# Quarters instead of halves: layer norms, adaptive scale and shift, and residual sums of an eight-stage transformer chain

## The chip, the cores and the metric

The kernel runs on one core of a Trainium2 chip. The metric is the device time of one execution in microseconds; the time before is 1702.09, the median of three runs (1697.55 to 1703.14). All arithmetic is in float32. A core has a tensor engine (PE, with its weight loads PEld), a vector engine (DVE), a scalar engine (ACT), GpSimd (POOL) and a queue that issues DMAs (SP). Matrix products land in PSUM; the rest of the data is in SBUF, 128 partitions wide.

## The reference, cut to what matters

1024 tokens (16 batches of 64) with 128 features pass through eight stages, each on the layer norm of the sum so far (residual):

```python
x = x + L0_xcond(_layernorm(x), cond, ctx)  # an attention decoder, recurrent over the 64 positions
x = x + L0_ffn(_layernorm(x))               # MoE, 8 experts, top 2, a shared expert, layer norm at its end
x = x + L1_xcond(ctx, _layernorm(x), cond)  # perceiver attention, 16 heads
x = x + L1_ffn(_layernorm(x))               # gated feed-forward with fake quantisation
x = x + L2_xcond(_layernorm(x), cond, ctx)  # six layers, below
x = x + L2_ffn(_layernorm(x))               # MoE, 8 experts, top 2
x = x + L3_xcond(_layernorm(x), cond, ctx)  # one block: two attentions of 16 heads, gated feed-forward
x = x + L3_ffn(_layernorm(x))               # MoE, 8 experts, top 2
```

The part that the change touches most is the adaptive layer norm, which the reference of the six layers writes as

```python
def _adaln(x, emb, w, b):
    gb = emb[:, 0, :] @ w.T + b
    g, be = jnp.split(gb, 2, axis=-1)
    return _ln(x) * (1.0 + g[:, None, :]) + be[:, None, :]
```

Scale and shift differ by batch and feature. Each layer applies it three times: before self attention, before cross attention and before the feed-forward. A few stages norm an input that is already a norm (the residual starts from `_ln(x)`), so that the second norm can be worked out from the first one's statistics; the kernel calls that "twice".

## The kernel before, in words

**Stages and planner.** Each stage builds a list of operations (`plan.op(engine, ns, emit, deps, takes, on, peers)`): the engine, an estimated duration, a function that emits the instructions, what must be done before, and a buffer that it takes. A greedy planner (`_Plan.order`) repeatedly emits, of all ready operations, the one that can start first by these durations; among equals the one with the longest remaining chain behind it goes first. Every engine then runs its instructions in the order of emission. The planner's durations only set the order: the waits between engines are put in afterwards, from what the instructions read and write. `peers` order starts only; `on` says that an operation works in another's buffer.

**Tiling.** Tokens lie on partitions in eight groups of 128 (`NT`). All planned stages work by halves of the tokens (512, four groups), `h` = 0 and 1, whose operations the planner interleaves. A half of feature-major data is one PSUM tile of 128x512, a whole bank. PSUM buffers of the layers: `pj` two tiles for nearly every product and transpose, `S` one of four banks for scores, `O` one of two banks for attention outputs. The block and the perceiver have four `pj`. The MoE stages have three `pj`, three `y`, two `tp`.

**A norm of a half** (`half_stats`, `half_scaled`, `half_features`, `adaln_half`): DVE takes statistics of four groups (L2137), aggregates them (L2143) and adds epsilon (L2144); POOL raises to the power -1/2 (L2148, four columns); DVE works out the shift (L2150); two groups are scaled by ACT (L2179) and two by DVE (L2177) into `xn`; PE transposes all four into one PSUM tile (L2192); DVE multiplies it by the scale into `xT` (L2202, 128x512) and POOL adds the shift (L2204). Every user of `xT` waits for that POOL addition.

**Attention in the layers** (`attend_half`): q, its rotated copy, k and v are projected from `xT` through `pj`; DVE and POOL rotate (L2218, L2221); ACT and DVE spread q into `qx` by masks (L2266, L2268); PE makes scores into `S`, ACT exponentiates (L2300), PE makes outputs into `O`, in four groups `p`, of which 0 and 1 lie in the first bank of `O` and 2 and 3 in the second. After groups 0 and 1, and again after 2 and 3, DVE takes reciprocals (L2309) and normalises (L2313), PE transposes, ACT copies, PE projects, and DVE adds to the residual (L2326), each time for a quarter of the tokens. The second add waited for the first (`last`), and the next norm waits for the second.

**Feed-forward of the layers** (`ffn_half`): four products with gelu on ACT (L2346), then `project`, one operation of 16 products into one `pj` tile, then one DVE add over the half (L2359). `glu_half` of the block does the same with a gate.

**MoE** (`moe`): for each expert and half four up-projections with activation, four down-projections (one per token group, 0.9 us each in the planner) into one `y` tile, and `weigh`: four DVE operations (L1674), one per group, that add the tile times the router's weight to the accumulator. `weigh` waits for all four down-projections.

**Heads of block and perceiver** (`heads_half`): the output projection is four operations of eight products into one `pj` tile, then one DVE add (L1884).

**Layers' start.** `norm_half` (L1331 to L1344) norms the stage's input into the residual, emitted before the plan; the first layer's norm then starts from that result.

Of the kernel before, what the change touches and what calls it, by code (L numbers as in the profile page):

```python
# [1140 lines left out]
class _Plan:  # L1141
# [13 lines left out]
    def op(self, engine, ns, emit, deps=(), takes=None, on=None, peers=(), table=None):  # L1155
# [3 lines left out]
        o.k, o.users, o.slot = len(self.ops), [], None  # L1159
        deps = list({id(d): d for d in deps if d is not None}.values())  # L1160
# [84 lines left out]
class _Fast(_Net):  # L1245
# [319 lines left out]
    NORM = (("st", 4, [128, 4, 6]), ("mv", 4, [128, 4, 3]), ("rs", 4, [128, 4, 6]), ("xn", 2, [128, 4, D]))  # L1565
# [3 lines left out]
    def moe(self, name, act, gated=False, shared=False):  # L1569
# [7 lines left out]
        with ExitStack() as st:  # L1577
# [29 lines left out]
            for h in range(2):  # L1607
                t = self.half_features(self.half_norm(half(x0, h), None), "tp")
                xTs.append(plan.op("ACT", 600, lambda _, h=h, t=t: nc.scalar.copy(
                    xT[:, h * 512:(h + 1) * 512], t.slot[1]), [t]))  # L1610
# [22 lines left out]
            for h in range(2):  # L1633
# [3 lines left out]
                for e in ([E] if shared else []) + list(range(E)):  # L1637
# [28 lines left out]
                    def weigh(y, e=e, h=h, acc=acc, first=last is None):  # L1666
                        for k in range(4):
# [9 lines left out]
                    last = plan.op("DVE", 1300, weigh, [*downs, None if e == E else route, last], on=y)  # L1677
                    if e == 1:
                        t = plan.op("PE", 870, lambda t, h=h: self.mm(t, cT, bd[:, h * 512:(h + 1) * 512]), [cTo], "tp")
                        last = plan.op("DVE", 690, lambda _, t=t, acc=acc: nc.vector.tensor_tensor(  # L1680
                            acc.rearrange("p k d -> p (k d)"), acc.rearrange("p k d -> p (k d)"), t.slot[1], ALU.add),
                            [t, last])
                if shared:
# [4 lines left out]
                    xa, xb = self.half_norm(acc, last)  # L1688
                    g = plan.op("DVE", 690, lambda t: nc.vector.tensor_tensor(t, t, row("ln_g"), ALU.mult),
                                [xa, xb], on=xa)  # L1690
                    plan.op("DVE", 690, lambda _, h=h, g=g: nc.vector.tensor_tensor(
                        half(x, h), half(x, h), g.home.slot[1], ALU.add), [g, base])
# [63 lines left out]
    def heads_half(self, h, x, wq, wk, wv, wo, inv, q, ks, vs, many, bias, top):  # L1756
# [118 lines left out]
        ys = []  # L1875
# [8 lines left out]
        return plan.op("DVE", 690, lambda t: nc.vector.tensor_tensor(flat, flat, t, ALU.add), [*ys, top], on=y)  # L1884

    def perceiver(self):
# [5 lines left out]
        with ExitStack() as st:  # L1892
# [12 lines left out]
            wide = [128, 8, T]  # L1905
            view = lambda v: v.rearrange("p (b t) -> p b t", t=T)
            deps = []
            for h in range(2):
                bs, part = slice(h * 8, (h + 1) * 8), slice(h * 4, (h + 1) * 4)
                t = self.half_features(self.half_norm(self.ctx[:, part, :], None))  # L1910
                c = plan.op("DVE", 690, lambda _, t=t, bs=bs: nc.vector.tensor_scalar(
                    kvT[:, bs, 0, :], view(t.slot[1]), w("ln1_w"), w("ln1_b"), ALU.mult, ALU.add), [t])
                xh = x0[:, part, :]
                t = self.half_features(self.half_scaled(xh, self.half_stats(xh, None, True)[1], 3))
                l = plan.op("DVE", 690, lambda _, t=t, bs=bs: nc.vector.tensor_tensor(
                    kvT[:, bs, 1, :], view(t.slot[1]), a[:, bs].unsqueeze(2).to_broadcast(wide), ALU.mult), [t])
                l = plan.op("POOL", 1060, lambda _, bs=bs: nc.gpsimd.tensor_tensor(
                    kvT[:, bs, 1, :], kvT[:, bs, 1, :], b[:, bs].unsqueeze(2).to_broadcast(wide), ALU.add), [l])
# [17 lines left out]
    def block(self):  # L1936
# [4 lines left out]
        with ExitStack() as st:  # L1941
# [13 lines left out]
            for h in range(2):  # L1955
# [6 lines left out]
                once, twice = self.half_stats(x0h, None, True)  # L1962
                firsts.append(self.half_scaled(x0h, twice, 3))
                xa, xb = self.half_scaled(x0h, once, 0, xh)
# [165 lines left out]
    def half_stats(self, x, top, twice=False):  # L2130
# [22 lines left out]
        if not twice:  # L2153
            return once
# [276 lines left out]
```

## Time and profile before

| what | us |
|---|---|
| median of the three runs | 1702.09 |
| the profiled execution, whole | 1709.73 |
| its span, first to last instruction | 1707.9 |
| stretch 0 to 230: decoder | PE busy 197.6 |
| 230 to 374: first MoE | PE busy 130.4 of 144 |
| 374 to 526: perceiver | PE busy 144.9 of 152 |
| 526 to 594: quantised feed-forward | PE busy 38.8 of 68 |
| 594 to 1218: six layers | 624 |
| 1218 to 1346: second MoE | 128 |
| 1346 to 1573: block | PE busy 215.6 of 227 |
| 1573 to 1708: third MoE and end | PE busy 122.0 of 135 |

One layer in the middle takes 95.6 us (886.6 to 982.2), of which PE is busy 82. A matrix product of 128x512 takes 0.59 us in the record and about 1.2 where the granted clock of the tensor engine is 0.5; the clock is given as a share of full speed. Products are pipelined, so that the records of two in a row overlap.

How to read the profile: a group or timeline line names the engine, the line of the kernel, the operation, the tile written and the tiles read, shapes and count; in brackets stands how long the engine had been idle before and which engine's instruction ended that. L295 is the line of a helper that issues every product, so products are told apart by their tiles. The windows give busy time of each engine in a stretch, and the mean clock. The list of waits gives, for an engine, the total of idle times that a certain instruction of another engine ended.

### The profile page before, as it was taken

To read this page: it belongs to the slowest core of one execution; us is meant where nothing else is said; L and a number is where in the kernel's file an instruction comes from. 1 tells how busy PE (TensorE), PEld (TensorE's weight loads), DVE (VectorE), ACT (ScalarE), POOL (GpSimd) and SP (SyncE) were. 2 spreads that over 40 slices of the span, in tenths; PEclk is the share of its full clock that TensorE was granted. 3 is DMA by queue.
4 is the path that set the end of the run, shared out by engine and by line. 5 is a ranking of instruction groups with operands and counts; after the bars stand their busy time and mean duration, and the time that the engine had idled before them with its cause. 6 is when DMAs were issued, how large, how long until landed. Compare 5 with 4: busy or idle time off the path is not lost.

```text
span 1707.9 us, 46734 instructions
## 1 busy us (share of the span) xinstructions
PE 1510.6 (88%) x21223; PEld 1113.3 (65%) x21223; DVE 711.0 (42%) x2217; ACT 533.6 (31%) x885; POOL 206.3 (12%) x210
## 2 busy tenths in 40 slices
PE   6999979969996698888798888888899899998997
PEld 5888857757774256566566556566567678775675
DVE  4434441243335565545646554444311343443212
ACT  2111134433321123333343333323343333332432
POOL 0000000020000032312222231212100200001000
PEclk7555569989997689989999897765799899999999
DMA  6000000000000040101000000000300200000000
GB/s 219 4 4 4 5 1 1 1 1 1 2 2 9 12 174 17 29 16 30 16 7 16 16 16 12 19 2 2 131 7 1 100 2 2 2 2 1 1 1 15
DMA packets 14332, 38.41 MB, mean 22 GB/s; under 512 B 1682, under 2 KB 6674, under 8 KB 14125
## 3 DMA queue, kind: packets, MB, share of 16 engines
q1 hardware_dynamic: 14125, 35.34, 6.1%
q8 instruction: 168, 2.75, 0.7%
q14 instruction: 39, 0.32, 0.1%
HBM read 34.81 MB, written 0.52 MB: 21 GB/s over the span
## 4 chain that ended last, share of the span: by engine, by line
PE 59%; DVE 11%; issue 3%; POOL 2%; ACT 2%; DMA 0%; DVEq 0%; ACTq 0%; POOLq 0%; SPq 0%
PE pj L295 35%; PE O L295 8%; PE y L295 7%; PE S L295 6%; DVE qx L2268 2%; DVE u L2218 1%; PE pj L1865 1%; DVE st L2137 1%; ACT P L2300 1%; POOL xT L2204 1%; POOL rs L2148 1%; DVE mv L2144 1%; PE pj L2319 1%; PE tp L295 1%; DVE xT L2202 1%
## 5 line engine op out<-in xcount | busy, mean ns | idle before, releaser
L295 PEld LDWEIGHTS y<-m_sb,H 128*128 128x128 f32 x1568 | 185.8, 192 | 32.5 <-issue 31.3
L295 PE MATMUL pj<-xT,m_sb 128*128 128x512 f32 x392 | 189.6, 618 | 0.0
L295 PE MATMUL y<-m_sb,H 128*128 128x128 f32 x1568 | 186.0, 275 | 0.0
L2300 ACT ACTIVATE P<-S 128x1024 f32<-128x1024 f32 x96 | 98.1, 1022 | 164.1 <-PE S L295 164.1
L1650 ACT ACTIVATE H<-pj,m_sb 128x512 f32<-128x512 f32 x128 | 87.5, 687 | 130.6 <-PE pj L295 130.3
L295 PEld LDWEIGHTS pj<-xT,m_sb 128*128 128x128 f32 x392 | 72.2, 199 | 63.3 <-issue 63.1
L2148 POOL TENSOR_TENSOR rs<-mv,minus_half 128x4 f32<-128x4 f32 x54 | 56.2, 1045 | 464.9 <-DVE mv L2144 463.8
L1674 DVE SCALAR_TENSOR_TENSOR x<-y,cw,x 128x128 f32<-128x128 f32 x128 | 36.0, 344 | 174.6 <-PE y L295 174.6
L2218 DVE TENSOR_TENSOR u<-pj,consts_sb 128x512 f32<-128x512 f32 x96 | 65.7, 688 | 68.7 <-PE pj L295 68.0
L2179 ACT ACTIVATE xn<-x,rs 128x128 f32<-128x128 f32 x100 | 43.4, 485 | 95.4 <-DVE rs L2150 78.4
L295 PE MATMUL pj<-xT,w_sb 128*128 128x512 f32 x128 | 66.3, 639 | 3.5 <-POOL xT L2204 3.1
L1775 DVE COPY QKV<-pj 128x512 f32<-128x512 f32 x56 | 38.6, 690 | 73.9 <-PE pj L295 73.8
L295 PE MATMUL pj<-xT,l_f 128*128 128x512 f32 x96 | 56.7, 720 | 13.7 <-POOL xT L2204 6.0
L295 PE MATMUL cb<-bd,E 128*32 128x2 f32 x4096 | 64.9, 192 | 2.9 <-issue 2.9
L1650 ACT ACTIVATE H<-pj,b1g,m_sb 128x512 f32<-128x512 f32 x64 | 49.6, 777 | 53.8 <-PE pj L295 50.8
L295 PEld LDWEIGHTS O<-Vc,P 128*64 128x64 f32 x1536 | 59.5, 163 | 10.4 <-issue 8.3
L295 PE MATMUL O<-Vc,P 128*64 128x18 f32 x1536 | 64.5, 230 | 0.0
L295 PEld LDWEIGHTS cb<-bd,E 128*32 128x32 f32 x4096 | 62.5, 156 | 3.0 <-issue 3.0
L2204 POOL TENSOR_TENSOR xT<-xT,ada 128x512 f32<-128x512 f32 x42 | 43.7, 1042 | 169.0 <-DVE xT L2202 130.7
L2192 PE MATMUL pj<-consts_sb,xn 128*128 128x128 f32 x184 | 36.4, 334 | 28.5 <-POOL rs L2148 14.6
L295 PE MATMUL S<-qx,krc 32*64 32x128 f32 x1536 | 42.0, 338 | 21.4 <-DVE qx L2268 17.8
L295 PE MATMUL O<-Vs,P 128*64 128x18 f32 x1536 | 55.4, 217 | 5.4 <-DVE On L2313 5.4
(363 smaller groups left out, 2617.2 us busy)
## 6 DMA issues: line engine op xcount, KB each, us to landing
w_sb<-in_w SPq DMA_DIRECT2D x7, 681.5 KB, 8.3
m_sb<-in_m SPq DMA_DIRECT2D x8, 515.0 KB, 6.6
m_sb<-in_m SPq DMA_DIRECT2D x8, 514.5 KB, 6.1
m_sb<-in_m SPq DMA_DIRECT2D x7, 565.5 KB, 9.4
l_f<-in_l SPq DMA_DIRECT2D x6, 578.5 KB, 3.9
l_a<-in_l SPq DMA_DIRECT2D x6, 387.0 KB, 3.1
l_s<-in_l SPq DMA_DIRECT2D x6, 384.0 KB, 3.2
w_sb<-in_w SPq DMA_DIRECT2D x4, 512.5 KB, 11.6
```

The lines of the kernel that those rows point to most:

```text
L295: self.nc.tensor.matmul(out, lhsT=lhsT, rhs=rhs, start=start, stop=stop, **kw)
L1650: nc.scalar.activation(a[:, c, :], ups[c].slot[1], act, bias=b, scale=g)
L1674: nc.vector.scalar_tensor_tensor(acc[:, k, :], src, g, x0[:, i, :] if first else acc[:, k, :], ALU.mult, ALU.add)
L1775: e(o, i.rearrange("p (b t) -> p b t", t=T) if len(o.shape) == 3 else i)
L1865: t = plan.op("PE", 700, lambda t, On=On: [nc.tensor.transpose(t[:, i * 128:(i + 1) * 128], On.slot[1][:, i * 128:(i + 1) * 128], self.ide ...
L2148: rs = plan.op("POOL", 1030, lambda t: nc.gpsimd.tensor_tensor(t[:, :, 0], at(mv, 2), self.minus_half[:, 0:4], ALU.pow), [mv], "rs")
L2179: nc.scalar.activation(o, x[:, k, :], AF.Identity, bias=b, scale=r)
L2192: return self.plan.op("PE", 900, lambda t: [self.nc.tensor.transpose(t[:, k * 128:(k + 1) * 128], xa.slot[1][:, k, :], self.ident) for k i ...
L2204: return plan.op("POOL", 1060, lambda a: nc.gpsimd.tensor_tensor(view(a), view(a), part(2 * n + 1), ALU.add), [m, ada], on=m)
L2218: us.append(plan.op("DVE", 690, lambda u, t=t, k=k, table=table: nc.vector.tensor_tensor(view(u[:, k, :]), view(t.slot[1]), self.c(table). ...
L2268: nc.vector.tensor_scalar(o, r, m, None, ALU.mult)
L2300: P = plan.op("ACT", 1030, lambda P, S=S: nc.scalar.activation(P.rearrange("p (g c) -> p g c", g=4), S.slot[1][:, :, 0:256], AF.Exp, scale ...
```

## The change

- `half_stats`, `half_scaled` and `adaln_half`'s two operations go. A new `quarter_norm` norms two token groups: statistics, aggregates and epsilon as one DVE operation, the power on POOL over two columns, the shift on DVE, then one group on ACT and one on DVE. With `twice` it also gives the second norm's factors; with `out` the first norm's result is written as well.
- `half_features` transposes by quarters into the two halves of one PSUM tile and calls `use` for each. `adapted` is that use for adaptive norms: for each batch of 64 tokens one operation `x * scale + shift` with the scale and shift as columns, read from PSUM, two batches of a quarter on ACT and two on DVE. POOL's addition goes.
- The residual sums of `ffn_half` and `glu_half` (new `add_quarters`), of `heads_half`, and the MoE's `weigh` are split in two, each waiting for its own products; norms wait for the add of their quarter. In the attention of the layers the second add no longer waits for the first.
- In the layers `norm_half` goes; the residual's start is written by `quarter_norm` with `out`, inside the plan. The perceiver, the block and the MoE's last norm use the same functions.

```diff
-    NORM = (("st", 4, [128, 4, 6]), ("mv", 4, [128, 4, 3]), ("rs", 4, [128, 4, 6]), ("xn", 2, [128, 4, D]))
+    NORM = (("nq", 6, [128, 2, 16]), ("xn", 4, [128, 2, D]))
...
-                    last = plan.op("DVE", 1300, weigh, [*downs, None if e == E else route, last], on=y)
+                    last = [plan.op("DVE", 650, lambda y, j=j, weigh=weigh: weigh(y, j), [
+                        *downs[2 * j:2 * j + 2], None if e == E else route, last and last[j]], on=y)
+                        for j in range(2)]
...
-        return plan.op("DVE", 690, lambda t: nc.vector.tensor_tensor(flat, flat, t, ALU.add), [*ys, top], on=y)
+        for k in range(2):
+            cut = slice(k * 256, (k + 1) * 256)
+            adds.append(plan.op("DVE", 420, lambda t, cut=cut: nc.vector.tensor_tensor(
+                flat[:, cut], flat[:, cut], t[:, cut], ALU.add), [*ys[2 * k:2 * k + 2], top], on=y))
+        return adds
...
+    def add_quarters(self, x, project, deps, base):
+        nc, plan = self.nc, self.plan
+        flat, t, adds = x.rearrange("p k d -> p (k d)"), None, []
+        for q in range(2):
+            cut = slice(q * 256, (q + 1) * 256)
+            o = plan.op("PE", 1800, lambda t, q=q: project(t, q), deps, None if q else "pj", on=t, peers=[t])
+            t = t or o
+            adds.append(plan.op("DVE", 420, lambda _, cut=cut: nc.vector.tensor_tensor(
+                flat[:, cut], flat[:, cut], t.slot[1][:, cut], ALU.add), [o, base]))
+        return adds
...
-            for h in range(2):
-                self.norm_half(x0, h, xs[h])
-            tops = [None, None]
+            qs = [[self.quarter_norm(x0[:, h * 4:(h + 1) * 4, :], k, None, True, xs[h]) for k in range(2)]
+                  for h in range(2)]
+            tops = [[o for _, o in qs[h]] for h in range(2)]
...
+    def quarter_norm(self, x, k, top, twice=False, out=None):
+        xk = x[:, 2 * k:2 * k + 2, :]
+        def stats(t):
+            for i in range(2):
+                nc.vector.bn_stats(out=t[:, i, 0:6], in_=xk[:, i, :])
+            for i in range(2):
+                nc.vector.bn_aggr(out=t[:, i, 6:8], in_=t[:, i, 0:6])
+            nc.vector.tensor_scalar(t[:, :, 8], t[:, :, 7], EPS, None, ALU.add)
...
+        q = plan.op("DVE", 1060, stats, [top], "nq")
+        r = plan.op("POOL", 1030, power(8, 9), [q], on=q)
+        once = plan.op("DVE", 180, shift(9), [r], on=q) if not twice or out is not None else None
...
+        n = plan.op("ACT", 480, lambda t: scaled("ACT", 0, at, t[:, 0, :]), [rs], "xn")
+        n = [n, plan.op("DVE", 350, lambda t: scaled("DVE", 1, at, t[:, 1, :]), [rs], on=n, peers=[n])]
...
+    def half_features(self, ns, use, kind="pj"):
+        plan, t, ops = self.plan, None, []
+        for k, n in enumerate(ns):
+            def transpose(t, k=k, n=n):
+                for i in range(2):
+                    at = (2 * k + i) * 128
+                    self.nc.tensor.transpose(t[:, at:at + 128], n[0].slot[1][:, i, :], self.ident)
+            o = plan.op("PE", 450, transpose, n, None if k else kind, on=t, peers=[t])
+            t = t or o
+            ops += use(k, lambda: t.slot[1], o)
+        return ops
...
+            for j, engine in enumerate(("ACT", "DVE")):
+                def run(a, j=j, engine=engine):
...
+                    for b in (2 * j, 2 * j + 1):
+                        f = scale()[:, 4 * k + b:4 * k + b + 1], shift()[:, 4 * k + b:4 * k + b + 1]
+                        if engine == "DVE":
+                            nc.vector.tensor_scalar(o[:, b, :], i[:, b, :], *f, ALU.mult, ALU.add)
+                        else:
+                            nc.scalar.activation(o[:, b, :], i[:, b, :], AF.Identity, bias=f[1], scale=f[0])
...
+                o = plan.op(engine, 700 if engine == "ACT" else 460, run, [t, ada], take if first else None,
...
-            last = plan.op("DVE", 420, lambda _, xv=xv, t=t: nc.vector.tensor_tensor(
-                xv, xv, t.slot[1][:, :256], ALU.add), [t, last])
+            adds.append(plan.op("DVE", 420, lambda _, xv=xv, t=t: nc.vector.tensor_tensor(
+                xv, xv, t.slot[1][:, :256], ALU.add), [t]))
...
-        t = plan.op("PE", 3550, project, [*hs, load], "pj")
-        flat = x.rearrange("p k d -> p (k d)")
-        return plan.op("DVE", 690, lambda _: nc.vector.tensor_tensor(flat, flat, t.slot[1], ALU.add), [t, xb])
+        return self.add_quarters(x, project, [*hs, load], xb)
```

## The prediction

> **What bounds the kernel now.** First the page, then busy time by stage, then the tensor engine's waits in the longest stage, then that stage's timeline.
>
> ```profile
> span 1707.9 us, 46734 instructions
> PE 1510.6 (88%) x21223; PEld 1113.3 (65%) x21223; DVE 711.0 (42%) x2217; ACT 533.6 (31%) x885; POOL 206.3 (12%) x210
> ```
>
> PE is the bound, with little room. The windows (columns: stretch, PE, PEld, DVE, ACT, POOL busy, clock, DMA) show where the room lies: the six layers, one MoE stage, and one moment of a layer.
>
> ```profile
> 594.00:1218.00 624.00, 537.28 (x8096) 370.68 (x8096) 323.56 (x931) 209.18 (x306) 157.87 (x148) 0.87 0.09 26
> 1218.00:1346.00 128.00, 124.13 (x689) 90.39 (x689) 29.27 (x113) 48.52 (x74) 2.19 (x5) 0.96 0.13 50
> 906.00:910.00 4.00, 2.68 (x9) 1.32 (x10) 3.74 (x8) 0.88 (x2) 2.06 (x3) 1.00 0.00 0
> 946.00:949.40 3.40, 0.00 (x1) 0.01 (x1) 3.30 (x9) 0.72 (x1) 2.52 (x2) 0.71 0.25 95
> 949.40:958.00 8.60, 8.41 (x104) 5.20 (x104) 2.15 (x5) 2.93 (x4) 1.07 (x2) 0.52 0.01 2
> ```
>
> The layers leave PE idle for 87 us and run at a mean clock of 0.87; the MoE stage is 97% PE. At 946.0 PE does nothing for 3.4 us, and the next 8.6 us run at half clock. What ended PE's waits in the layers (total, times, longest):
>
> ```profile
> PE S L295 <- DVE qx L2268: 22.2, 11, 3.5
> PE pj L295 <- POOL xT L2204: 13.0, 14, 3.0
> ...
> PE O L295 <- DVE On L2313: 5.4, 5, 1.1
> PE pj L2319 <- DVE xT L2202: 4.9, 9, 0.6
> ```
>
> The first is that 3.4 us hole: the scores of the cross attention's first half wait for a chain that starts at the self attention's last add. Its ends in the timeline:
>
> ```profile
> 934.54 0.42 DVE L2326 TENSOR_TENSOR x<-x,pj 128x256 f32<-128x256 f32 x1 [2.19 <-PE pj L295]
> 934.88 0.86 DVE L2137 BATCH_NORM_STATS2 st<-x 128x6 f32<-128x128 f32 x4
> ...
> 941.77 1.04 POOL L2204 TENSOR_TENSOR xT<-xT,ada 128x512 f32<-128x512 f32 x1 [4.37 <-DVE xT L2202]
> ...
> 949.40 1.16 PE L295 MATMUL S<-qx,krc 32*64 32x128 f32 x32 [3.50 <-DVE qx L2268]
> ```
>
> The third wait matters for the change. The O tile holds four groups of outputs; the reciprocal (L2309) needs groups 0 and 1 alone, group 3 needs nothing of it:
>
> ```profile
> 924.69 2.05 PE L295 MATMUL O<-Vs,P 128*64 128x18 f32 x64
> ...
> 926.78 0.36 DVE L2309 RECIPROCAL inv<-O 128x32 f32<-128x32 f32 x1 [2.80 <-PE O L295]
> 927.17 0.49 DVE L2313 TENSOR_TENSOR On<-O,inv 128x128 f32<-128x128 f32 x2
> ...
> 927.81 1.11 PE L295 MATMUL O<-Vs,P 128*64 128x18 f32 x32 [1.07 <-DVE On L2313]
> ```
>
> The x64 is groups 1 and 2. DVE waits for group 2, and group 3 waits for DVE: writers and readers of one PSUM tile go in program order, whatever columns they touch. The change makes quarters inside PSUM tiles, so this is priced throughout.
>
> **The change, part by part** (us; plus is slower).
>
> Norm chain, from the last add to xT. Now: statistics and aggregates 1.3 (0.86, then 0.36 overlapping, 0.17), power 1.02 with 0.25 of hops, shift 0.24, two ACT rows 0.87, hop 0.15, transposes 0.66, xT multiply 0.69, POOL add 1.04, hops 0.2: 6.4; the trace took 7.85 from 934.96 to 942.81. After, for the last quarter: 0.9 for half the statistics, power 1.27 with hops, 0.24, one ACT row 0.48, 0.15, two transposes 0.44, then the feature scale and shift in pieces of 64 columns. On ACT such a piece is 0.43: the xn row 128x128 at 0.485 less 64 columns of 0.9 ns (copies of 512 and 256 columns: 0.586 and 0.368); two in a row 0.76. On DVE it is 0.28, a second 0.20 later, from the 0.344 and the spacing of L1674's four (1.12 together): 0.48. No row has ACT and DVE read one tile at once; side by side it is 0.76, in order 0.76+0.1+0.48. I take in order, as the O tile goes. Sum 4.9: a gain of 1.5. The power of 2 columns instead of 4 is not shown: 0.51 (half) to 1.02; I take 1.02, the nearer row's. Where is it exposed? In the hole at the cross attention's first half, six times: **-9** (-4 to -14).
>
> After the feed-forward both adds come together. The second quarter's transposes then wait for the first quarter's readers: add 0.8, statistics to 1.75, first transposes done at 4.25, its readers at 5.75, second at 7.8, against 7.2 now. One half per layer has no cover: 6 x 0.6 = **+3.6** (-9 to +8).
>
> The clock. Idle of 3.4 us was followed by 8.41 us of PE work at half clock, which is 4.2 lost; with holes of 1.0 to 1.2 us at 906 the clock stayed at 1.00. A hole of 3.4-1.5 = 1.9 lies between; I take half of it over five layers: **-10.5** (0 to -21). The Trainium skill (TensorE: Matmul & The Clock Gate, HAM oscillation) says that only idle beyond about 3.4 us drops the clock; by that rule alone this term would be -21.
>
> MoE sums by halves of y. L1674's four operations become two and two, the first pair due after two of four down projections. The planner places it between the third and the fourth. In program order it waits for the third, and the fourth waits for it: 0.05+0.61+0.15 = 0.8 of PE idle in a stage without slack. That happens only where the four run back to back. With halves, the chain of sums costs 690 per expert by the planner's numbers instead of 1340, so in the second half an up-projection two experts ahead outranks the down projections and splits them, as in the first half now. What is left is the last three experts and the one at the bias matmul: 4 or 5 per stage, 14 in all: **+11** (0 to 39, all 49 groups). The last sum of a stage is half as long: **-1.5**.
>
> Output projections of the heads: the first add falls between the third and fourth block: 0.05+0.42+0.15 = 0.6, six halves: **+3.6** (0 to 3.6). Feed-forward sums by quarters: PE writes both before DVE's first add, which waits for both; two adds take 0.8 instead of 0.69: 14 x 0.1 = **+1.4**. That part does not do what it says.
>
> pj in the layers has two buffers. Now xT's tile is held for 0.66+0.1+0.69+0.15 = 1.6. After, from the first quarter's transposes to the second's readers: the adds lie 2.6 apart (931.93, 934.54), plus 0.44+0.1+0.76+0.1+0.48: 4.5, or 2.8 times. PE waits today 4.9+1.5 = 6.4 for that reader; the increase is 1.8 x 6.4 = **+11.5** (0 to 23).
>
> DVE and ACT. Per half DVE gives up 0.69 and gets 0.96 of pieces and a second shift and epsilon (0.2 each in a row): +0.6. It also waits for ACT's two pieces, 0.86 per quarter; u, qx and the adds stand behind it. ACT gets 4 x 0.4 and, at 31% busy, hides it; if exponentials stand ahead, DVE waits longer. DVE is the bound only in 906 to 910 (3.74 of 4 us), one half a layer: 6 x 2.3 = 13.8. Against it: small DVE operations stall behind the POOL add (mv at 904.60 took 0.83 against a median of 0.17, ending with it); that excess is 4.6 in the kernel, and no such excess lies under a power. **+9** (0 to 14). POOL itself trades one add for a second power, 1.04 for 1.02, in the slack of a 12% engine.
>
> Stage starts: MoE's first norm about 1 earlier, three times: **-3**. Norms taken twice (perceiver, block, layers) need eight powers instead of four, but the first half needs four either way: 0. The layers' own first norm (L1331 to L1344, emitted ahead of the plan) moves into it and shares its statistics: eight statistics of 0.28 and their aggregates less on DVE between 595 and 602, behind them the masks that POOL's V columns wait for; PE is then mostly waiting for weights (half clock, DMA landing), so 0. All three together -10 to +8.
>
> Sum: -9+3.6-10.5+11-1.5+3.6+1.4+11.5+9-3 = +16. The profiled execution took 1709.7, 1.8 more than its span, and is 7.6 above the median; on the median of 1702.1 that is **1718**.
>
> The skill speaks against this change: PSUM — Partial Sum Buffer (PSUM bank collisions raise a hardware error) has two engines on one bank ordered by semaphores, two readers included. The O rows agree for PE and DVE; for two readers no run here shows it. Without that rule for readers, the chain gains 0.58 more, -3.5 over six layers.
>
> **Rivals.** *The clock holds (faster).* If the hole falls under the 1.2 us that 906 shows harmless, the clock term is -21, and the last half layer, at 0.63 from 1125 to 1218, gains too: 0.74 of its 80 us of PE time is at half clock, 59, so 30 are lost; half of that back is -15. 1718-10.5-15 = **1692**; with pj and DVE covered by PE's 14% of idle, down to 1672. For: 22.2 us wait on this one chain. Against: pj and DVE lengthen the same chain. 0.38.
>
> *Every MoE group stalls.* If the order stays four in a row, 49 x 0.8 = 39 instead of 11: **1746**. For: today's second halves run in fours. Against: the ranks above. 0.15.
>
> *Gains and stalls cancel.* If PE's idle in the layers (87 us) hides the pj and DVE terms, 20.5, and nothing else changes: 1718-20.5 = **1698**, within what can be told from no change. For: most of that idle stands outside the hole. Against: DVE's 94% from 906 to 916 has no room. 0.10.
>
> **How the numbers follow.** Forecast 1718 with 0.37 (its own range 1707 to 1735). Slower: 0.37+0.15 = 0.52; faster 0.38; same (within 0.3%, 5 us, which is about what the three runs can tell) 0.10. The sums of all bounds reach 1650 and 1790; not all fall one way, so the range is 1668 to 1752.
>
> **What would show it.** Right: y matmuls waiting for DVE x or acc in the MoE stages, about 14 times 0.8; adapted DVE pieces that begin when ACT's end; PE waits for xT's readers well above 6.4; the hole before S near 2 us. Wrong: ACT and DVE pieces overlapping, fourth down projections without a gap, or the layers at a clock above 0.93: then the faster case holds.

## The result, and the profile after

The change makes the kernel slower by 0.6%: 1711.23 us (median of four runs, 1710.87 to 1713.71) against 1702.28 for the kernel before on the same chip (four runs, 1697.55 to 1703.14), ratio 1.0061, 95% interval 1.0041 to 1.0082. The profiled execution took 1713.71, its span 1711.9. From the page of the changed kernel:

```profile
span 1711.9 us, 47383 instructions
...
PE 1505.3 (88%) x21223; PEld 1102.8 (64%) x21223; DVE 758.1 (44%) x2509; ACT 596.5 (35%) x1069; POOL 183.5 (11%) x226
...
L2241 DVE TENSOR_SCALAR xT<-pj,ada 128x64 f32<-128x64 f32 x168 | 49.3, 339 | 60.7 <-ACT xT L2243 46.3
L2243 ACT ACTIVATE xT<-pj,ada 128x64 f32<-128x64 f32 x168 | 58.7, 402 | 45.4 <-PE pj L2215 32.3
```

PE is busy 5 us less than before, and yet the span is 4 us longer. The windows by stage say where (changed kernel; columns as before: stretch, PE, PEld, DVE, ACT, POOL busy, clock, DMA; stages are cut at their last sum):

```profile
225.70:377.50 151.80, 136.73 (x727) 98.08 (x727) 43.23 (x157) 60.48 (x83) 7.54 (x10) 0.93 0.00 1
...
607.60:1203.80 596.20, 521.21 (x8096) 357.91 (x8096) 346.97 (x1126) 260.29 (x450) 136.03 (x151) 0.91 0.09 27
1203.80:1338.00 134.20, 123.93 (x669) 88.62 (x669) 31.39 (x111) 47.76 (x73) 2.76 (x4) 0.95 0.12 44
...
1568.00:1702.70 134.70, 124.47 (x669) 88.88 (x669) 31.34 (x112) 49.15 (x74) 2.87 (x5) 0.95 0.00 1
```

Cut in the same way, the kernel before spent 142.4, 621.9, 127.1 and 127.0 in these four. So two large amounts nearly cancel: the layers give 25.7, and the three MoE stages take 9.4 + 7.1 + 7.7 = 24.2. The rest: decoder +1.9 (its code is untouched), perceiver +2.2, quantised feed-forward -0.6, block +1.9.

In the layers PE's waits are now these (total, times, longest):

```profile
PE pj L295 <- ACT P L2401: 13.0, 23, 0.8
PE S L295 <- DVE qx L2323: 10.6, 6, 1.9
...
PE pj L295 <- ACT xT L2243: 5.9, 9, 2.0
```

The wait for qx was 22.2 in 11 with 3.5 the longest. It has halved, and the hole before the cross attention's scores is now 1.72 to 1.89. PE's work is shorter by 16.1 (537.3 to 521.2, clock 0.87 to 0.91) and its idle by 9.6 (84.6 to 75.0). Against this, the first line was less than half as long before:

```profile
PE pj L295 <- ACT P L2346: 6.1, 9, 1.2
```

P is the gelu of the feed-forward, which reads a `pj` tile; when it is done, the tile is free again. The section on the prediction comes back to this wait. What is left of the hole is seen in the timeline of the second layer:

```profile
770.32 1.27 POOL L2276 TENSOR_TENSOR qr<-u 128x512 f32<-128x512 f32 x1 [0.41 <-DVE u L2273]
770.42 1.19 DVE L2171 SCALAR_TENSOR_TENSOR nq<-nq 128x2 f32<-128x2 f32 x1
771.53 0.47 DVE L2162 BATCH_NORM_STATS2 nq<-x 128x6 f32<-128x128 f32 x2
...
772.59 1.27 DVE L2323 TENSOR_SCALAR qx<-qr,consts_sb 128x512 f32<-128x512 f32 x3
...
773.91 0.37 PE L295 MATMUL S<-qx,krc 32*64 32x128 f32 x8 [1.72 <-DVE qx L2323]
```

qr is ready at 771.59, but DVE takes the other half's norm first: a shift that takes 1.19 instead of 0.16 because it starts under POOL's add, then statistics, and qx only at 772.59.

In the MoE stages the wait that the prediction named is there (second MoE stage; PE, DVE, PE):

```profile
1281.40 1.95 PE L295 MATMUL y<-m_sb,H 128*128 128x128 f32 x16
...
1283.39 0.61 DVE L1682 SCALAR_TENSOR_TENSOR x<-y,cw,x 128x128 f32<-128x128 f32 x2 [6.40 <-PE y L295]
...
1284.05 2.05 PE L295 MATMUL y<-m_sb,H 128*128 128x128 f32 x16 [0.70 <-DVE x L1682]
```

Two down projections (x16), two sums, and PE waits 0.70 for them before the other two. Of all y products, PE's waits are (total, times):

```profile
  DVE x L1682: 9.8, 14
  DVE acc L1682: 5.6, 8
  DVE acc L1680: 1.4, 2
```

24 stalls, 16.8 us. The first product behind each took 0.38 where 0.275 is the median. The kernel before has none.

### The profile page after: what moved, and what is told of

The parts are those of the page before. It is cut to its first block, busy times and chain, and to the rows that moved or that the text cites. A ratio compares the mean times of both kernels' runs of the same rounds, so it can differ in the third digit from the quotient of the medians.

```text
span 1711.9 us, 47383 instructions
## 1 busy us (share of the span) xinstructions
PE 1505.3 (88%) x21223; PEld 1102.8 (64%) x21223; DVE 758.1 (44%) x2509; ACT 596.5 (35%) x1069; POOL 183.5 (11%) x226
## 4 chain that ended last, share of the span: by engine, by line
PE 81%; DVE 10%; ACT 4%; issue 2%; DMA 1%; POOL 0%; SPq 0%; ACTq 0%; DVEq 0%; POOLq 0%
PE pj L295 40%; PE y L295 11%; PE O L295 9%; PE S L295 7%; PE cb L295 3%; PE hh L295 3%; PE lg L295 3%; PE pj L1878 1%; ACT xT L2243 1%; PE su L295 1%; DVE u L2273 1%; ACT P L2401 1%; DVE nq L2162 1%; PE pj L2215 1%; PE tp L295 1%
## 5 line engine op out<-in xcount | busy, mean ns | idle before, releaser
L295 PE MATMUL y<-m_sb,H 128*128 128x128 f32 x1568 | 193.5, 276 | 16.8 <-DVE x L1682 9.8
L2168 POOL TENSOR_TENSOR nq<-nq,minus_half 128x2 f32<-128x2 f32 x120 | 84.6, 710 | 611.1 <-DVE nq L2165 575.9
L2355 ACT ACTIVATE P<-S 128x1024 f32<-128x1024 f32 x96 | 98.1, 1022 | 119.1 <-PE S L295 118.8
L2198 ACT ACTIVATE xn<-x,nq 128x128 f32<-128x128 f32 x100 | 48.4, 490 | 123.9 <-DVE nq L2171 123.4
L2241 DVE TENSOR_SCALAR xT<-pj,ada 128x64 f32<-128x64 f32 x168 | 49.3, 339 | 60.7 <-ACT xT L2243 46.3
L2243 ACT ACTIVATE xT<-pj,ada 128x64 f32<-128x64 f32 x168 | 58.7, 402 | 45.4 <-PE pj L2215 32.3
L2215 PE MATMUL pj<-consts_sb,xn 128*128 128x128 f32 x184 | 41.3, 320 | 31.1 <-ACT xn L2198 20.1
L295 PE MATMUL pj<-xT,l_s 128*128 128x512 f32 x96 | 55.9, 692 | 9.9 <-DVE u L2273 6.9
L1845 ACT ACTIVATE P<-S 128x1024 f32<-128x1024 f32 x32 | 32.8, 1025 | 84.8 <-PE S L295 84.5
L1534 ACT ACTIVATE H<-hh 128x16 f32<-128x16 f32 x64 | 12.9, 202 | 138.9 <-PE hh L295 138.9
## 6 DMA issues: line engine op xcount, KB each, us to landing
w_sb<-in_w SPq DMA_DIRECT2D x4, 512.5 KB, 11.9
```

The source lines that it names most:

```text
L295: self.nc.tensor.matmul(out, lhsT=lhsT, rhs=rhs, start=start, stop=stop, **kw)
L1845: P = plan.op("ACT", 1030, lambda P, S=S: nc.scalar.activation(P.rearrange("p (j n) -> p j n", j=2), S.slot[1], AF.Exp, scale=0.125), [o f ...
L2168: return lambda t: nc.gpsimd.tensor_tensor(t[:, :, b], t[:, :, a], self.minus_half[:, 0:2], ALU.pow)
L2198: nc.scalar.activation(o, xk[:, i, :], AF.Identity, bias=f[1], scale=f[0])
L2215: self.nc.tensor.transpose(t[:, at:at + 128], n[0].slot[1][:, i, :], self.ident)
L2241: nc.vector.tensor_scalar(o[:, b, :], i[:, b, :], *f, ALU.mult, ALU.add)
```

## The experiments

Each is compared with the kernel before on its own chip (medians there 1707.9 for the first four, 1708.1 for the second four, then 1711.2, and 1707.3 for the last). Stage times are those of the one profiled execution; where two kernels have the same layers, these differ by up to 4.4 (581.6 and 586.0, 593.7 to 596.5). Whole times can differ by more between executions of one kernel (half_norms_old_scale: 1683.3 to 1706.5), so the ratios are the firmer figures.

| kernel | median | ratio, 95% | layers | three MoE | perceiver | block |
|---|---|---|---|---|---|---|
| before | 1702.3 | 1 | 621.9 | 396.5 | 163.1 | 228.1 |
| changed | 1711.2 | 1.0061 (1.0041 to 1.0082) | 596.2 | 420.7 | 165.4 | 229.9 |
| moe_one | 1692.3 | 0.9911 (0.9885 to 0.9937) | 596.4 | 397.6 | 166.3 | 229.9 |
| moe_late | 1692.1 | 0.9907 (0.9879 to 0.9935) | 593.7 | 397.4 | 166.3 | 231.4 |
| moe_one_heads_one | 1694.9 | 0.9923 (0.9898 to 0.9949) | 596.5 | 397.9 | 165.8 | 231.9 |
| before_moe_halves | 1733.1 | 1.0150 (1.0102 to 1.0198) | 621.7 | 418.6 | 162.8 | 228.4 |
| half_norms | 1781.0 | 1.0406 (1.0370 to 1.0441) | 687.3 | 399.4 | 166.3 | 228.3 |
| old_scale | 1674.7 | 0.9797 (0.9781 to 0.9814) | 586.0 | 399.3 | 166.3 | 227.1 |
| transposes_together | 1775.0 | 1.0380 (1.0358 to 1.0401) | 680.9 | 397.3 | 170.1 | 228.8 |
| engine_per_quarter | 1692.2 | 0.9910 (0.9885 to 0.9936) | 585.6 | 398.1 | 166.6 | 228.9 |
| half_norms_old_scale | 1696.3 | 0.9898 (0.9836 to 0.9960) | 610.5 | 399.5 | 166.4 | 225.6 |
| pieces_dve_only | 1688.3 | 0.9875 (0.9855 to 0.9895) | 586.1 | 395.6 | 170.2 | 227.5 |
| old_scale_ffn_one | 1686.9 | 0.9863 (0.9838 to 0.9888) | 593.2 | 396.6 | 166.6 | 227.0 |
| perceiver_halves | 1671.3 | 0.9788 (0.9766 to 0.9810) | 581.6 | 397.7 | 163.8 | 227.3 |

### MoE sums: the wait, or the order of the work?

**moe_one**: the changed kernel with the sums undone.

```diff
-  last = [plan.op("DVE", 650, lambda y, j=j, ...: weigh(y, j),
-                  [*downs[2 * j:2 * j + 2], ..., last and last[j]], on=y) for j in range(2)]
+  o = plan.op("DVE", 1300, lambda y, ...: (weigh(y, 0), weigh(y, 1)), [*downs, ..., last], on=y)
+  last = [o, o]
```

> The changed kernel, its MoE sums again one operation of four sums after all four down projections; norms, feature scale and shift and feed-forward sums stay changed. The three MoE stages took 142.4, 127.1, 127.0 us before and 151.8, 134.2, 134.7 after, 24.2 more in all. If the split sums cost that (theory), the stages come back to 142 +-1.5, 127 +-1, 127 +-1 and the time to 1687 (1711.2 - 24.2), faster than both. If the quarter norms and the split copies at the start of each stage cost it (rival A), they stay near 152, 134 and 135 and the time stays at 1711. The layers should stay at 596 +-3 in both cases.

The MoE stages came back to 140.8, 128.4 and 128.4, and the layers stayed; 0.9911 of 1702.3 is 1687. The theory held, rival A fell.

**moe_late**: two operations still, but each due only after all four down projections.

```diff
-                  [*downs[2 * j:2 * j + 2], None if e == E else route, last and last[j]], on=y)
+                  [*downs, None if e == E else route, last and last[j]], on=y)
```

> The changed kernel with the MoE sums still in two operations of two sums, but both depending on all four down projections, so that in the program the first pair comes after the fourth down projection. As many DVE operations as in the changed kernel. If waits cost the 24.2 us, that is, the fourth (or third) down projection waiting for the sums of the same y tile (theory): stages within 1.5 us of those with one operation, time 1687 to 1689, and no wait of a y matmul for DVE x or acc of the 24 that took 16.8 us. If it is what the planner's shorter chain of sums does to the order of up and down projections, or the number of operations (rival B): stages stay 5 to 9 us longer each, 1705 to 1711.

Its timeline, at the place that answers to the one above:

```profile
1266.59 3.73 PE L295 MATMUL y<-m_sb,H 128*128 128x128 f32 x32
...
1269.47 1.13 DVE L1682 SCALAR_TENSOR_TENSOR x<-y,cw,x 128x128 f32<-128x128 f32 x4 [6.77 <-PE y L295]
```

Four down projections run without a gap (x32), no y product waits for DVE anywhere, and stages and time are those of moe_one. As many operations and the same shorter chain of sums as in the changed kernel, and nothing lost: the place of the sums between the writers of their tile is the cost. Rival B fell.

**before_moe_halves**: the kernel before with the split sums alone (the first diff, the other way round).

> The kernel before with this part of the change alone: MoE sums in two operations of two, the first after two of four down projections. Theory: the three MoE stages get 7 to 9.5 us longer each, 24 in all, the layers stay at 622 +-3, time 1702.3 + 24 = 1726. By the prediction's count (14 stalls of 0.8) 1713. Rival A (the stage starts cost it): 1702.

The stages grew by 9.4, 6.3 and 6.4, 22 in all, the layers stayed at 621.7, and the ratio of 1.015 on 1708 is 25.6 us (17 to 34 by its interval). The same step, 1.0061 less 0.9911, is lost between moe_one and the changed kernel.

### The sums behind the heads

**moe_one_heads_one**: also one add of 512 columns there.

```diff
-  for k in range(2):
-      adds.append(plan.op("DVE", 420, ..., [*ys[2 * k:2 * k + 2], top], on=y))
+  o = plan.op("DVE", 690, lambda t: nc.vector.tensor_tensor(flat, flat, t, ALU.add), [*ys, top], on=y)
```

> MoE sums in one operation, and the sum behind the output projections of the perceiver's and the block's heads too (one add of 512 columns after all four blocks, instead of two adds of 256). By the prediction's term of 0.6 us for each of six halves the perceiver is 1.2 and the block 2.4 shorter than with the MoE sums alone undone, 3.6 in all: 1683 to 1684. If the halves hide it (rival), both stages are within 1 us and the time within 2 us of that kernel.

The perceiver is 0.5 shorter and the block 2.0 longer, where the rival allowed 1; but the block of moe_late, the same as that of moe_one, is 1.5 longer too, and the intervals of the ratios overlap. So no gain from undoing it is found. In the changed kernel only three of the six halves show the wait (0.5 each).

### The layers: norms and scale, two by two

**half_norms**: from moe_one, norms of layers and block over four rows of tokens (but for the layers' and the block's first).

```diff
-  ns = ns or [self.quarter_norm(x, k, tops[k]) for k in range(2)]
+  ns = ns or self.whole_norm(x, tops)
```

> From the kernel with the MoE sums in one operation (1692.3 us, layers 596.4, before 621.9). In the layers and the block, the norms again by halves: statistics of four rows, one power of four columns, two rows on ACT and two on DVE; the layers' and the block's first norm, the transposes by quarters and the feature scale and shift in pieces on ACT and DVE stay. By the prediction's chain the quarter saves 0.9 of the 1.5 us (half the statistics, one ACT row, two transposes), the scale and shift 0.6. Theory 1 (the quarter norm is the larger part of the layers' gain of 25.7): layers 608 to 618, time 1704 to 1714. Theory 2 (what earns it is the POOL add that is gone): layers 594 to 600, time 1690 to 1696.

**old_scale**: from moe_one, quarter norms, but the multiply and the POOL add of the kernel before.

```diff
-  return self.half_features(ns, self.adapted("xT", part(2 * n), part(2 * n + 1), ada))
...
+      m = plan.op("DVE", 690, lambda a: self.nc.vector.tensor_tensor(
+          view(a), view(psum()), part(2 * n)().unsqueeze(2).to_broadcast(wide), ALU.mult), [*ts, ada], "xT")
+      return [plan.op("POOL", 1060, lambda a: self.nc.gpsimd.tensor_tensor(
+          view(a), view(a), part(2 * n + 1)().unsqueeze(2).to_broadcast(wide), ALU.add), [m, ada], on=m)]
```

> The other way round, from the same kernel (1692.3, layers 596.4): norms and transposes by quarters, but the feature scale and shift in layers and block as before, one DVE multiply of 512 columns after both quarters' transposes and one POOL add of 512 columns. Theory 1 (quarter norms earn most): layers 600 to 606, time 1696 to 1702. Theory 2 (the POOL add's removal earns most): layers 612 to 622, time 1708 to 1718. If the two only work together (the hole must fall under some length to keep the clock), both this kernel and the one with half norms lose 15 or more.

**half_norms_old_scale**: both diffs together.

> The fourth cell of a table: MoE sums in one operation, norms of layers and block by halves, and the feature scale and shift there by one DVE multiply and one POOL add. What is left of the change in the layers is the adds of the feed-forward by quarters. The cells so far (layers): quarter norms with pieces 596, quarter norms with multiply and add 586, half norms with pieces 687; the kernel before 622. If the quarter norms earn the gain (theory), the layers lie at 615 to 630 and the time at 1703 to 1718. If half norms as written here are slow for another reason than the pieces (rival: the order of the work that comes of them), the layers lie above 640 and the 687 says little about the pieces.

Both first expectations missed, by far and in opposite directions. The four cells, as ratios with the layers in brackets:

| | multiply and add | pieces on ACT and DVE |
|---|---|---|
| half norms | 0.9898 (610) | 1.0406 (687) |
| quarter norms | 0.9797 (586) | 0.9911 (596) |

Quarter norms gain 1.0% beside the old scale and shift. The pieces, which the prediction's chain had as a gain, lose 1.1% beside quarter norms and 5% beside half norms: neither theory had them as a loss. The fourth cell lies below its 615 to 630 and far from the rival's 640, so half norms as such do not explain the 687. Where it goes is seen in the timeline at the cross attention of the fourth layer (half_norms):

```profile
998.70 1.26 POOL L2303 TENSOR_TENSOR qr<-u 128x512 f32<-128x512 f32 x1
998.77 1.22 DVE L2275 SCALAR_TENSOR_TENSOR nh<-nh 128x4 f32<-128x4 f32 x1 [0.60 <-POOL nh L2273]
1000.02 0.88 ACT L2284 ACTIVATE xn<-x,nh 128x128 f32<-128x128 f32 x2 [6.83 <-DVE nh L2275]
...
1000.57 1.29 PE L2215 MATMUL pj<-consts_sb,xn 128*128 128x128 f32 x4 [3.40 <-ACT xn L2284]
...
1001.89 0.70 ACT L2243 ACTIVATE xT<-pj,ada 128x64 f32<-128x64 f32 x2 [0.38 <-PE pj L2215]
1002.63 1.10 DVE L2241 TENSOR_SCALAR xT<-pj,ada 128x64 f32<-128x64 f32 x4 [1.21 <-ACT xT L2243]
...
1003.76 0.70 ACT L2243 ACTIVATE xT<-pj,ada 128x64 f32<-128x64 f32 x2 [1.17 <-DVE xT L2241]
1004.51 2.08 PE L295 MATMUL pj<-xT,l_q 128*128 128x512 f32 x2 [2.66 <-ACT xT L2243]
```

Read it down the engines. ACT does its two pieces, DVE waits 1.21 for them and does four, ACT waits 1.17 for those and does its last two: 2.57 from 1001.89 to 1004.46, where one multiply and one add are 0.69 + 1.04 and a hop, 1.9. PE stands for 3.40 before the transposes and 2.66 behind them. Only the second hole is the pieces' turns. Some 1.05 of the first is the shift at 998.77, which took 1.22 because POOL's add had begun; in half_norms_old_scale the shift at this place came before the add, and PE waited 1.52:

```profile
948.37 0.17 DVE L2287 SCALAR_TENSOR_TENSOR nh<-nh 128x4 f32<-128x4 f32 x1
948.51 1.27 POOL L2315 TENSOR_TENSOR qr<-u 128x512 f32<-128x512 f32 x1 [0.18 <-DVE u L2312]
```

So the 5% is the pieces together with the order of work that came with them; no run tells the two apart. In half_norms such a pair of holes lies in six places, one per layer. What follows them (window of half_norms, same columns):

```profile
1004.50:1018.00 13.50, 12.24 (x206) 8.23 (x206) 3.51 (x8) 3.91 (x5) 1.26 (x1) 0.50 0.01 2
```

13.5 us at half clock. In its layers PE is idle for 124.3 and its work takes 563.0 at a mean clock of 0.83; for half_norms_old_scale it is 78.4, 532.1 and 0.89, for old_scale 64.1, 521.9 and 0.91.

Beside quarter norms, where the pieces lose 1.1%, the same rival stands. In moe_one and in the changed kernel six shifts, one per layer, take 1.18 to 1.19 under POOL's add before the cross attention's scores; in old_scale the longest of all 116 is 0.36. Against it speaks pieces_dve_only (below), which has five such shifts and layers of 586.1.

### What of the pieces costs

**transposes_together**: from moe_one, all four transposes in one operation, so that pj is held for a shorter time.

```diff
-  o = plan.op("PE", 450, transpose, n, None if k else kind, on=t, peers=[t])
+  t = plan.op("PE", 900, transpose, ns, kind)
```

> From the same kernel: all four transposes of a half in one operation after both quarters' norms, so that the pj tile is held from there on and not from the first quarter's transposes; the pieces of scale and shift are unchanged. The prediction priced the longer hold of pj at +11.5. If that is paid, time 1681 to 1688 (layers 585 to 592). If it is hidden by PE's idle time (rival), the first quarter's head start is lost instead and the layers get 0 to 8 longer, 1692 to 1700.

Neither: the layers took 680.9. With both quarters of xT coming at once, the pieces again run in turns, PE waits for them 2.66 to 2.81 in every layer before the cross attention's queries, and the clock falls to 0.82. So the staggering of the quarters seems to hide the pieces' turns in the changed kernel. What the longer hold of pj costs this run can't tell: it takes the staggering away together with the hold.

**engine_per_quarter**: ACT takes the first quarter, DVE the second.

```diff
-  for j, engine in enumerate(("ACT", "DVE")):
+  for engine in ("DVE" if k else "ACT",):
...
-          for b in (2 * j, 2 * j + 1):
+          for b in range(4):
```

> From the same kernel: ACT does all four pieces of the first quarter, DVE all four of the second, instead of two each in both. In the changed kernel DVE stood idle 46.3 us in 43 stretches that an ACT piece ended. If the order of the two readers of one quarter costs time on the path (theory): the last quarter takes four DVE pieces, 0.34 + 3 x 0.2 = 0.94 instead of 0.8 (two on ACT) + 0.1 + 0.54, 0.5 less, at 12 to 24 halves 1686 to 1690; DVE idle ended by ACT xT falls under 10 us. If the first quarter's four ACT pieces (4 x 0.40 = 1.6) now hold back the second quarter's transposes (rival): +0.5 to +0.8 per half, 1695 to 1705.

DVE's waits in the layers (total, times, longest), first moe_one, then this kernel:

```profile
DVE xT L2241 <- ACT xT L2243: 41.1, 36, 3.1
```

```profile
DVE xT L2241 <- ACT xT L2243: 16.9, 7, 2.9
```

The waits went from 36 to 7, and the median did not move. Nine of the ten runs lie between 1680.8 and 1693.5, one at 1710.2, and the profiled one, with layers of 585.6, was the fastest of them: inconclusive on the layers, but these waits of DVE are not what the changed kernel loses by at the median.

**pieces_dve_only**: all pieces on DVE.

```diff
-  for j, engine in enumerate(("ACT", "DVE")):
+  for engine in ("DVE",):
...
-          for b in (2 * j, 2 * j + 1):
+          for b in range(4):
```

> MoE sums in one operation, quarter norms, the feature scale and shift in pieces of 64 columns, but all four of a quarter on DVE. DVE gets 22 us more to do in the layers (36 halves x 4 pieces less the 4 that overlap, 4 x 0.2 = 0.8 each half less what waiting is gone), ACT 58 less (144 x 0.40). If the cost of the pieces against multiply and add (596 against 586, 1692 against 1675) is ACT's place in the chain and the order of the two readers (theory): 586 to 590, time 1674 to 1683. If it is the number of small operations on DVE (rival): layers 597 to 612, time 1693 to 1708.

Layers of 586.1 as the theory had it, in an execution that was the fastest of four (1681.2); the median, 1688.3, lies between the two cases, and the perceiver is 3.9 longer than in moe_one. It doesn't decide how the loss is shared between ACT's place in the chain and DVE's small operations (DVE is busy 381.8 in these layers, 347.2 in moe_one).

### Feed-forward sums, and the perceiver

**old_scale_ffn_one**: one projection and one add in the feed-forwards of layers and block, and the old scale and shift in the perceiver too.

```diff
-  for q in range(2):
-      o = plan.op("PE", 1800, lambda t, q=q: project(t, q), deps, None if q else "pj", on=t, peers=[t])
...
-      adds.append(plan.op("DVE", 420, ..., [o, base]))
+  t = plan.op("PE", 3550, lambda t: (project(t, 0), project(t, 1)), deps, "pj")
+  o = plan.op("DVE", 690, ..., [t, base])
```

> From the fastest kernel so far (quarter norms, multiply and add in layers and block, MoE sums in one operation; 1674.7, layers 586.0, perceiver 166.3, block 227.1): in the perceiver too the feature scale and shift as before, and in all feed-forwards one down projection of 16 matmul groups and one add of 512 columns again. Perceiver: 163 to 164 if the pieces cost its 3 us (theory), 166 if the quarter norms do. Feed-forwards: in the trace both adds stand behind all 32 matmuls, so the prediction's term says the two adds bring nothing and cost 0.1 each, 1.2 in the layers: layers 584 to 586, time 1670 to 1673. Rival: the first add and its statistics between the two adds bring the first quarter forward by 0.3 to 0.9 at each of 12 halves: layers 590 to 597, time 1676 to 1683.

The rival held: layers of 593.2 against 586.0 and 581.6, and a ratio of 0.9863 against old_scale's 0.9797, intervals apart. PE stands 2.36 before the cross attention's scores in all six layers here, and in two of six in old_scale. The perceiver stayed at 166.6, so its pieces are not its loss. The two forms that the quarters take, first in old_scale:

```profile
709.03 3.84 PE L295 MATMUL pj<-l_f,P 128*128 128x128 f32 x32
...
712.97 0.42 DVE L2030 TENSOR_TENSOR x<-x,pj 128x256 f32<-128x256 f32 x1 [3.29 <-PE pj L295]
...
713.43 0.49 DVE L2162 BATCH_NORM_STATS2 nq<-x 128x6 f32<-128x128 f32 x2
...
714.24 0.41 DVE L2030 TENSOR_TENSOR x<-x,pj 128x256 f32<-128x256 f32 x1
```

The first add waits for all 32 products, as predicted, but the first quarter's statistics run before the second add. And in the changed kernel:

```profile
1091.62 2.05 PE L295 MATMUL pj<-l_f,P 128*128 128x128 f32 x16 [0.56 <-ACT P L2401]
...
1093.78 0.42 DVE L2030 TENSOR_TENSOR x<-x,pj 128x256 f32<-128x256 f32 x1 [2.08 <-PE pj L295]
...
1094.37 1.95 PE L295 MATMUL pj<-l_f,P 128*128 128x128 f32 x16
```

Here an up projection stands between the two halves, and the first add comes 2.6 before the second. In the changed kernel that is so for the first half of all six layers, in old_scale for two halves of twelve.

**perceiver_halves**: old_scale, with the perceiver's norms, transposes and scale and shift of the kernel before (its half_stats, half_scaled and the two operations behind them put back for that stage).

> From the fastest kernel so far (1674.7 on a chip where the kernel before took 1708.1, ratio 0.980), with the perceiver's norms and scale and shift as in the kernel before, by halves. The perceiver took 163.1 before and 166.3 to 166.6 with quarter norms, whether the scale and shift was in pieces or not. If the quarter norms cost that (theory: eight statistics, powers and shifts where there were four, in a stage whose start PE waits out), the perceiver takes 162 to 164 and the ratio is 0.978. If it is something else, 166 and 0.980. The layers, untouched, lie at 582 to 590 in both cases.

163.8: the quarter norms, with their transposes, cost the perceiver its 3 us. The ratio of 0.9788 can't be told from old_scale's 0.9797. This is the fastest version, 2.1% below the kernel before and 2.7% below the changed one (0.9788 / 1.0061).

## Why the prediction was right, and where not

The sign and the time (1718 against 1711.2) were right, but by luck: two errors largely cancel. The MoE term was too small by 13 to 15, and the layers' sum, +6 where -25.7 was measured, too large by some 30. Of the signs that the prediction named, four came: the y products' waits, DVE's pieces that begin when ACT's end (46.3 us of DVE's idle, L2241 above), the hole near 2 us, and a clock of 0.91, not above 0.93. Longer waits for xT's readers did not come under that name.

The layers can be taken apart by the table, in single executions: 621.9 before, 610.5 with the rest of the change but half norms and the old scale and shift, 586.0 with quarter norms, 596.4 with the pieces.

- **MoE sums by halves (+11): mechanism shown, size too small.** The stall was priced at 0.8 and is that (0.70 of idle and a first product 0.1 longer). Its number was wrong: 24, not 14. The step that failed is "What is left is the last three experts and the one at the bias matmul": more groups stay in fours than the ranks led one to think. 24 x 0.8 is 19; against moe_late it is 23 (420.7 - 397.4); the other 4 were not traced to a wait. The rival in which every group stalls bore the right mechanism with twice the number (49).
- **Norm chain (-9) and clock (-10.5): right in kind.** The hole fell from 3.50 to 1.72 to 1.89 where 1.9 was foreseen; idle fell by 9.6 and PE's work by 16.1. The four cells show that quarter norms gain and that the POOL add's going does not: with the old scale and shift they take the layers from 610.5 to 586.0 (idle 78.4 to 64.1, work 532.1 to 521.9) and the whole by 1.0%. They are not the whole gain: 11 of the layers come before them, from 621.9 to 610.5.
- **Feed-forward sums (+1.4, "That part does not do what it says") and what follows them (+3.6): wrong sign.** This step failed. The text was right on six halves of twelve in the changed kernel. On the others the add does come early, and undoing all of it, beside the old scale and shift, costs 7 in the layers (593.2 against 586.0) and 0.7% in all (0.9863 against 0.9797).
- **The scale and shift in pieces: a loss, as the sum had it, but not by its terms.** The chain took 1.93 to 1.34 for them, a gain; the terms for pj and for DVE and ACT were the price. With the norms held fixed the pieces lose 10 in the layers and 1.1%, beside half norms 5%. The chain's gain is not seen: it prices one quarter by itself, 0.76 + 0.1 + 0.48, and in half_norms ACT and DVE pass their waits on to each other. Whether that, the shift under POOL's add or the hold of pj makes the 1.1% is open. (The power, 0.69 at the median instead of the 1.02 taken, was a term too large by 0.3.)
- **pj held longer (+11.5), DVE and ACT (+9): seen, not sized.** In the trace the tile of xT's transposes is held for a median of 1.6 before and 4.4 after, as foreseen (1.6 and 4.5). PE's wait does not stand at xT's readers (5.9 for ACT's, 6.4 before for DVE's) but at those of the other tile, which products must then share. PE's waits for the gelu went from 6.1 to 18.0. Of these 11.9 stand before products and transposes that need a free tile (5.0 before the change), the rest before products that read the gelu's result. In the changed kernel:

```profile
711.66 0.44 PE L2215 MATMUL pj<-consts_sb,xn 128*128 128x128 f32 x2 [0.71 <-ACT P L2401]
711.93 1.02 PE L295 MATMUL pj<-xT,l_f 128*128 128x512 f32 x2
...
712.99 0.69 ACT L2401 ACTIVATE P<-pj,l_f 128x512 f32<-128x512 f32 x1 [0.16 <-PE pj L295]
...
713.73 1.12 PE L295 MATMUL pj<-xT,l_f 128*128 128x512 f32 x2 [0.78 <-ACT P L2401]
...
715.81 0.70 ACT L2243 ACTIVATE xT<-pj,ada 128x64 f32<-128x64 f32 x2 [0.22 <-DVE xT L2241]
```

  From 711.66 to 716.51 one tile is xT's, and the product at 713.73 waits for the gelu to free the other. No run changes the hold alone, so what it costs in time stays open.
- **Heads' projection (+3.6): not found.** Three waits of 0.5, and no gain from undoing it.
- **Stage starts (-3), norms taken twice (0): wrong by little.** With the sums undone the MoE stages are 1.1 longer than before, not 3 shorter, and the perceiver 3 longer by its quarter norms.

The Trainium skill (TensorE: Matmul & The Clock Gate, HAM oscillation) has the clock drop behind idle gaps beyond about 3.4 us. Here shorter ones cost too, but not each time. The hole of 1.72 shown above, and the same hole two layers later (958.2), have these windows (changed kernel; before and behind the first, behind the second):

```profile
772.30:773.90 1.60, 0.00 (x0) 0.00 (x0) 1.60 (x7) 0.51 (x1) 1.00 (x1) 1.00 0.17 61
773.90:782.00 8.10, 7.89 (x150) 5.37 (x152) 4.60 (x11) 4.49 (x8) 0.57 (x1) 0.79 0.09 26
...
959.90:968.00 8.10, 6.71 (x159) 4.44 (x160) 4.58 (x11) 4.62 (x8) 0.81 (x1) 1.00 0.01 2
```

Of four holes of 1.72, those at 772.2 and 864.7 were followed by a mean clock of 0.79, those at 958.2 and 1050.4 by 1.00. In the kernel before, a hole of 1.07 at 733.7 was followed by half clock as well (735.8 to 739.2), while those of 1.0 to 1.2 at 906 were not. So here the measurement decides: gaps of half the page's length can cost, and the prediction's half of the clock term was nearer than none. But the length of a gap alone does not settle it, and what does was not tested.

## What to carry to other kernels

Look where the first half of a halved operation lands. Between the writers of the tile that it reads, it cost 1.5% here; the same two operations behind the last writer cost nothing. A chain that is shorter on paper can lose: one engine's multiply and a third engine's add were 1.1% faster than pieces shared by two engines, and 5% where both quarters came at once, though the reason is only in part known. And a change of many parts should be run part by part: this one held a gain of 2% that two of its own parts ate.

## What the runs showed of the hardware that was not expected

- DVE's shift of two inputs from SBUF took 1.18 to 1.19 instead of 0.16 all six times that it started 0.1 after POOL's 128x512 add (L2276), and ended within 0.1 of it. Fourteen shifts that lay wholly under a POOL power of 128x2 took 0.15 to 0.16. The Trainium skill (SBUF — State Buffer, SBUF: two separate sides) has DVE operations with two SBUF inputs wait for the whole of a GpSimd operation that reads SBUF; the adds agree, the powers don't.
- A POOL power of 128x2 has a median of 0.69, one of 128x4 in the kernel before 1.02. From these two, an estimate is 0.36 and 0.165 for each column.
- A pair of holes of 3.40 and 2.66 was followed by 13.5 us at half clock, so that 6 us of idle cost about as much again.
